# A sandwich of a gated linear-attention block and a mixture of experts: two small GpSimd writes moved behind the making of the shares

## The chip, the cores and the metric

One NeuronCore of one Trainium2 chip runs the whole program in one launch. Its engines work side by side, each through its own instructions in a fixed order: TensorE (PE, matrix products and transposes), VectorE (DVE), ScalarE (ACT), GpSimd (POOL) and SyncE (SP, which mostly issues transfers). They wait for each other through semaphores. The metric is the device time of the program in microseconds (us); lower is better.

## The reference

2048 tokens of 256 channels go through two layers, each wrapped in the same way: the input is normalised, the layer is applied, its output is normalised and added to the input.

```python
x = x + _layernorm(attention_block(_layernorm(x)))     # 16 heads, gated memory along the tokens, then a gated MLP of 1024
x = x + _layernorm(moe(_layernorm(x)))

def moe(x):                                            # E = 8 experts of width 176, top 2; a shared expert of width 704
    shared = (silu(x @ sw_gate) * (x @ sw_up)) @ sw_down
    probs = softmax(x @ router_w.T)
    top_w, top_i = top_k(probs, 2);  top_w = top_w / sum(top_w)
    routed = sum over the two chosen experts e of top_w * ((silu(x @ w_gate[e]) * (x @ w_up[e])) @ w_down[e])
    return routed + sigmoid(x @ shared_gate_w) * shared
```

All of it is in float32.

## The kernel before

**Tiles.** The tokens are cut into `NB` = 8 blocks of 256; in a tile, 128 partitions hold `NT` = 2 groups of 128 tokens each. A block passes through small functions in turn: `enter` (first normalisation), `project`, `remember` and `leave` (the attention block; `leave` holds the second layernorm, `ln2_stats` and `ln2_norm`), `perceptron` (its MLP, eight chunks of the hidden width), `route` (normalisation ahead of the experts, choice of experts, places of the rows) and `shared` (the shared expert).

**The order around the change.** The functions of all blocks are cut into steps, and each step gets a place on one long line; the steps are sorted by place and recorded in that order, so that about four blocks are in work at a time. A recording layer then orders the instructions of each engine; it may put one earlier than it was written, where its data allow. Where the author wants none of that, `behind(engines)` (L107) holds what is recorded within it behind the last instruction recorded so far on these engines: an order edge on the same engine, without a semaphore.

**The route of a block.** `route(b)` makes the rows that go to the experts. Its tile `ln` (L761, tag `ln3`) has only two buffers, so block b + 2 uses the buffer of block b. A row has 339 columns: column 0 the number of the token's first pair (a pair is a token and one of its experts), column 1 the first expert, column 2 the share of the first expert, then the 256 normalised channels (from `X0`), 64 columns of the shared expert's tail (from `T0`), and 16 columns of zeros (from `ROW`). Who writes them:

- L764, ScalarE: the channels, by `normalize`
- L795, GpSimd: the copy of `first_pair` into column 0; L796, GpSimd: the memset of the last 16 columns
- L797, GpSimd: the share from `th`, a tanh on ScalarE; L798, GpSimd: the gate of the shared expert from the same `th`
- L800, GpSimd: the tail, `end` times the gate
- L805, GpSimd: the expert's number from `idf`

Then VectorE and TensorE count places, `rows` (L836) holds the row of each pair in the DRAM tensor `xs`, and four indirect transfers that GpSimd issues (L840) scatter the tile's rows there. When all blocks are through, the experts run over `xs` in 36 blocks of 128 rows (`routed`), scatter their results to `ys`, and the closing part adds all up.

**What else GpSimd does at that time.** It makes the inverse roots of the normalisations: `scale_of` (L328) adds the epsilon (L333) and takes the power -0.5 (L334) of a variance that VectorE has made (L322, L323). `normalize` (L337) goes on from there with a small product on VectorE (L341) and two activations on ScalarE (L343). GpSimd also adds the first layer's output to the input (L737) and clears a part of the experts' weights (L1134).

**What TensorE does.** In the stretch where the change lies its order is a dense row of products of `perceptron` (L389 into `psM`, L714 into `psD`) and `shared` (L389 into `psS` and `psA`), with transposes (L380) between. `psM` has three banks, which ScalarE and VectorE clear (L724, L725, and L767 for the transposes of `route`).

Of the kernel before, what the change touches and what calls it, by code (L numbers as in the profile page):

```python
# [16 lines left out]
DVE, POOL = mybir.EngineType.DVE, mybir.EngineType.Pool  # L17
# [10 lines left out]
def kernel(ctx: ExitStack, tc: tile.TileContext, a: dict, out: bass.AP):  # L28
    nc = tc.nc
# [16 lines left out]
    NT = TB // P  # L46
# [42 lines left out]
    ROW, H0 = T0 + TAIL, T0 - I  # L89
# [6 lines left out]
    first_pair = const.tile([P, NB * NT], F32, name="first_pair")  # L96
# [10 lines left out]
    def behind(*engines):  # L107

        traced, held = nc.cur_bb.bb.instructions, ExitStack()
        for engine in engines:  # L110
            last = next((i for i in reversed(traced) if i.engine == engine), None)
            if last is not None:
                held.enter_context(tc.issue_after(last))
        return held
# [643 lines left out]
    def route(b):  # L758

        t = live[b]  # L760
        ln = act.tile([P, NT, W], F32, tag="ln3", name=f"ln3_{b}", bufs=2)  # L761
# [30 lines left out]
        nc.vector.tensor_copy(th[:, :, 1], lg[:, :, E])  # L792
        nc.scalar.activation(th, th, AF.Tanh, scale=0.5)
        gate = small.tile([P, NT], F32, tag="gate", name=f"gate_{b}", bufs=NB)
        nc.gpsimd.tensor_copy(ln[:, :, 0], first_pair[:, b * NT : (b + 1) * NT])  # L795
        nc.gpsimd.memset(ln[:, :, ROW:], 0.0)  # L796
        nc.gpsimd.tensor_scalar(ln[:, :, 2], th[:, :, 0], 0.5, 0.5, ALU.mult, ALU.add)  # L797
        nc.gpsimd.tensor_scalar(gate, th[:, :, 1], 0.5, 0.5, ALU.mult, ALU.add)  # L798

        nc.gpsimd.tensor_tensor(  # L800
            ln[:, :, T0:ROW], end, gate.unsqueeze(2).to_broadcast([P, NT, TAIL]), ALU.mult
# [239 lines left out]
    def evenly(n):  # L1041
# [12 lines left out]
    runs = (  # L1054
        (perceptron, 3, (*range(NF), 7.8, 7.9, 8.6)),
        (route, 4, (1.4, 2.0, 4.2, 5.2, 5.3, 9.2, 10.2, 10.3)),
        (shared, NB + .9, evenly(NS + 3)),
    )
# [23 lines left out]
    for line in opening.split():  # L1082
        name, b = line.rsplit(":", 1) if ":" in line else (line, "0")
# [149 lines left out]
```

## Time and profile before

| | us |
|---|---|
| median of 3 runs | 529.25 (526.84 to 529.47) |
| the profiled execution | 530.06 |
| its span, first to last instruction | 528.2 |
| TensorE busy | 508.6 |
| VectorE busy | 331.4 |
| ScalarE busy | 216.9 |
| GpSimd busy | 171.5 |
| mean granted clock of TensorE | 0.991 |

The profile names operations by line of the kernel, engine, and tiles as `out<-in`. A timeline row is start, length, engine, line and operation; the brackets at its end give how long the engine sat idle before, and what ended that. The instructions of the two moved lines took 0.183 to 0.675 us (L795, median 0.186, 8 of them) and 0.117 to 0.129 us (L796, median 0.118, 8 of them). By the engine's waits, GpSimd waited ahead of L795 three times for scatters (11.4 us in all, the longest 6.0), twice with TensorE's product named last (3.7) and once with nothing named (2.0).

Where GpSimd has them in the profiled execution, with the block whose tile is written:

| block | L795 at us | what stands right ahead on GpSimd | the block's L805 at us |
|---|---|---|---|
| 0 | 51.24 | memset L302 | 127.90 |
| 1 | 107.94 | root L334 | 164.70 |
| 2 | 153.40 | scatters of block 0 | 200.76 |
| 3 | 188.42 | scatters of block 1 | 237.28 |
| 4 | 224.59 | scatters of block 2 | 267.75 |
| 5 | 257.90 | scatters of block 3 | 303.85 |
| 6 | 294.22 | scatters of block 4 | 339.34 |
| 7 | 329.73 | scatters of block 5 | 364.47 |

The memset L796 follows the copy at once; only block 0's stands apart, at 4.69 us, between the first two steps of the first normalisation.

### The profile page before, as it was taken

How to read it: one execution, taken by the hardware profiler on the slowest of the kernel's cores; microseconds unless marked ns; L12 is line 12 of the kernel's file. 1: busy time of each engine (PE TensorE's matmuls, PEld its weight loads, DVE VectorE, ACT ScalarE, POOL GpSimd, SP SyncE). 2: the span in 40 equal slices, each digit the busy share in tenths (PEclk: the TensorE clock that was granted, in tenths of full speed). 3: DMA queues.
4: the chain of work that ended last, by engine and by line, in shares of the span. 5: the costliest groups of instructions: out<-in, count | busy, mean ns of one | idle time of the engine just before them, and what ended most of it. 6: DMA issues, size and time to landing. Idle time of an engine off the chain costs nothing.

```text
span 528.2 us, 7925 instructions
## 1 busy us (share of the span) xinstructions
PE 508.6 (96%) x2468; PEld 423.1 (80%) x2468; DVE 331.4 (63%) x1100; ACT 216.9 (41%) x500; POOL 171.5 (32%) x309
## 2 busy tenths in 40 slices
PE   8999899999999999999899899999999999999992
PEld 5877687888878888888688788888877777778881
DVE  4788999887896997996754233235134444441983
ACT  4655454544644645543232323213124444443250
POOL 7233202213344341412314214025104334432551
PEclk9999999999999999999999999999999999999997
DMA  4981101001011001110102911002624344323621
GB/s 135 389 264 22 20 2 20 1 1 21 1 54 20 27 27 22 53 20 3 53 1 85 311 26 53 1 0 77 169 67 122 108 120 123 106 85 117 258 87 54
DMA packets 31793, 41.26 MB, mean 78 GB/s; under 512 B 4825, under 2 KB 26629, under 8 KB 31751
## 3 DMA queue, kind: packets, MB, share of 16 engines
q1 hardware_dynamic: 27888, 30.96, 20.5%
q0 software_dynamic: 3584, 9.79, 5.6%
q8 instruction: 20, 0.33, 0.3%
q14 instruction: 23, 0.18, 0.1%
q10 hardware_dynamic: 278, 0.01, 0.0%
HBM read 24.28 MB, written 15.15 MB: 75 GB/s over the span
## 4 chain that ended last, share of the span: by engine, by line
PE 44%; DVE 2%; POOL 2%; DMA 1%; issue 1%; ACT 1%; POOLq 0%; DVEq 0%
PE psM L389 19%; PE psD L389 7%; PE psA L389 6%; PE psS L389 4%; PE psD L714 3%; PE psA L950 1%; PE psB L978 1%; DMA xs<-ln,rows 1%; PE psB L389 1%; POOL xs L840 1%; POOL ln_rs L334 1%; DVE ln_st L322 0%; POOL x L737 0%; POOL ln_rs L333 0%; ACT h L343 0%
## 5 line engine op out<-in xcount | busy, mean ns | idle before, releaser
L389 PE MATMUL psM<-h2T,w_gate 128*128 128x256 f32 x256 | 67.5, 386 | 0.0
L389 PE MATMUL psM<-h2T,w_val 128*128 128x256 f32 x256 | 66.5, 381 | 0.0
L714 PE MATMUL psD<-w_out,hid 128*128 128x256 f32 x256 | 64.3, 381 | 0.1
L989 POOL DMA_INDIRECT ys<-yb,pair x36 | 35.4, 983 | 74.6 <-ACT yb L988 73.3
L389 PEld LDWEIGHTS psM<-h2T,w_gate 128*128 128x128 f32 x256 | 48.2, 192 | 8.3 <-DVE o L635 1.3
L389 PEld LDWEIGHTS psM<-h2T,w_val 128*128 128x128 f32 x256 | 49.0, 192 | 6.7
L714 PEld LDWEIGHTS psD<-w_out,hid 128*128 128x128 f32 x256 | 48.2, 190 | 7.4 <-DVE hid L725 1.2
L389 PE MATMUL psM<-m_w,xT 128*128 x144 | 48.7, 460 | 0.3 <-issue 0.3
L724 ACT ACTIVATE hid<-psM 128x256 f32<-128x256 f32 x64 | 23.7, 376 | 49.6 <-PE psM L389 49.5
L333 POOL TENSOR_SCALAR ln_rs<-ln_mv 128x2 f32<-128x2 f32 (+1 forms) x33 | 8.8, 268 | 104.4 <-DVE ln_mv L323 94.5
L725 DVE TENSOR_TENSOR hid<-hid,psM 128x256 f32<-128x256 f32 x64 | 26.1, 411 | 21.5 <-ACT hid L724 20.9
L840 POOL DMA_INDIRECT xs<-ln,rows x32 | 32.3, 1008 | 15.8 <-issue 7.2
L389 PE MATMUL psD<-m_w,hT 128*128 x144 | 37.2, 381 | 0.0
L389 PEld LDWEIGHTS psM<-m_w,xT 128*128 128x128 f32 x144 | 24.6, 191 | 8.2 <-issue 0.6
L389 PE MATMUL psA<-yT,s_gu 128*128 128x256 f32 x128 | 30.8, 381 | 0.0
L952 DVE COPY xT<-psA 128x256 f32<-128x256 f32 x36 | 15.3, 424 | 24.1 <-PE psA L950 24.1
L974 DVE TENSOR_TENSOR xb<-xb,psM 128x176 f32<-128x176 f32 x36 | 12.2, 338 | 26.9 <-ACT xb L973 26.9
L334 POOL TENSOR_TENSOR ln_rs<-ln_rs,neg_half 128x2 f32<-128x2 f32 (+1 forms) x33 | 26.0, 789 | 2.2
L389 PEld LDWEIGHTS psD<-m_w,hT 128*128 128x128 f32 x144 | 24.6, 191 | 2.4 <-ACT yb L988 0.5
L389 PEld LDWEIGHTS psA<-yT,s_gu 128*128 128x128 f32 x128 | 23.9, 190 | 3.0
L973 ACT ACTIVATE xb<-psM 128x176 f32<-128x176 f32 x36 | 11.4, 317 | 32.7 <-PE psM L389 31.8
L988 ACT ACTIVATE yb<-psD,share 128x256 f32<-128x256 f32 x36 | 17.0, 473 | 18.6 <-PE psD L389 18.4
(269 smaller groups left out, 1065.8 us busy)
## 6 DMA issues: line engine op xcount, KB each, us to landing
xb<-xs SPq DMA_DIRECT2D x36, 169.5 KB
g<-ys SPq DMA_DIRECT2D x8, 512.0 KB
xs<-zeros SPq DMA_DIRECT2D x16, 169.5 KB
x<-in_L_attn_x_dram SPq DMA_DIRECT2D x8, 256.0 KB
decay<-by_head SPq DMA_DIRECT2D x14, 128.0 KB
out_dram<-f SPq DMA_DIRECT2D x7, 256.0 KB
m_w<-in_L_ffn_w_gate_dram SPq DMA_DIRECT2D x2, 704.0 KB
m_w<-in_L_ffn_w_up_dram SPq DMA_DIRECT2D x2, 704.0 KB
```

What stands on the lines that cost most here:

```text
L333: nc.gpsimd.tensor_scalar(rs, mv[:, :, 1], EPS, None, ALU.add)
L334: roots.append(nc.gpsimd.tensor_tensor(rs, rs, neg_half[:, 0:nt], ALU.pow).ins)
L389: nc.tensor.matmul(po, lhs[i], rhs[i], start=(i == 0), stop=(i == len(lhs) - 1))
L714: nc.tensor.matmul(total[:, n * C : (n + 1) * C], hids[f][:, tok(n)], w_out[:, f, :], start=(f == 0 and n == 0), stop=(f == NF - 1 and n = ...
L724: nc.scalar.activation(hid, po[:, 0:TB], AF.Silu)
L725: nc.vector.tensor_tensor(hid, hid, po[:, TB:], ALU.mult)
L840: inst = nc.gpsimd.indirect_dma_start(out=xs, out_offset=bass.IndirectOffsetOnAxis(ap=rows[:, c : c + 1], axis=0), in_=ln[:, n, :], in_off ...
L952: nc.vector.tensor_copy(xT, pt[:, 0 : KC * P].rearrange("p (k t) -> p k t", k=KC))
L973: nc.scalar.activation(h[:, 0:I], po[:, 0:I], AF.Silu)
L974: nc.vector.tensor_tensor(h[:, 0:I], h[:, 0:I], po[:, I:GU], ALU.mult)
L988: nc.scalar.activation(yb, po[:, 0:C], AF.Copy, scale=share)
L989: inst = nc.gpsimd.indirect_dma_start(out=ys, out_offset=bass.IndirectOffsetOnAxis(ap=pair, axis=0), in_=yb, in_offset=None, bounds_check= ...
```

## The change

The copy L795 and the memset L796 are written behind the two makings L797 and L798, and inside `behind(POOL)`: the recording layer may not put them ahead of the gate of the same block.

```diff
         gate = small.tile([P, NT], F32, tag="gate", name=f"gate_{b}", bufs=NB)
-        nc.gpsimd.tensor_copy(ln[:, :, 0], first_pair[:, b * NT : (b + 1) * NT])
-        nc.gpsimd.memset(ln[:, :, ROW:], 0.0)
         nc.gpsimd.tensor_scalar(ln[:, :, 2], th[:, :, 0], 0.5, 0.5, ALU.mult, ALU.add)
         nc.gpsimd.tensor_scalar(gate, th[:, :, 1], 0.5, 0.5, ALU.mult, ALU.add)
+
+        with behind(POOL):
+            nc.gpsimd.tensor_copy(ln[:, :, 0], first_pair[:, b * NT : (b + 1) * NT])
+            nc.gpsimd.memset(ln[:, :, ROW:], 0.0)
 
         nc.gpsimd.tensor_tensor(
             ln[:, :, T0:ROW], end, gate.unsqueeze(2).to_broadcast([P, NT, TAIL]), ALU.mult
```

In the built program GpSimd then has, for each block: L805, L797, L798, the copy, the memset, L800. The wait for the scatters of block b - 2, which read the same buffer, stands at L805, now the first writer of the tile on GpSimd. TensorE, VectorE, ScalarE and SyncE have the same instructions in the same order with the same waits. (Lines below the change are two higher in the new program; the texts use the old numbers unless they say otherwise.)

## The prediction

> **What bounds the kernel now.** I read the page first (busy shares), then TensorE's own timeline for its idle time, then GpSimd's timeline around the moved lines, then the granted clock in one-microsecond stretches.
>
> ```profile
> PE 508.6 (96%) x2468; PEld 423.1 (80%) x2468; DVE 331.4 (63%) x1100; ACT 216.9 (41%) x500; POOL 171.5 (32%) x309
> ```
>
> TensorE sets the time: it is busy for 508.6 of 528.2 us, and its order is fixed. Every other engine matters only where TensorE stands still for it. Outside the first 90 us and the end it does so in few places; these five rows of its timeline (start, length, operation, and in brackets the idle time before and who ended it) are nearly all of it:
>
> ```profile
> 260.02 0.33 PE L380 MATMUL psB<-ident,ln 128*128 128x128 f32 x1 [1.20 <-ACT ln L343]
> 260.51 0.55 PE L380 MATMUL psB<-ident,ln 128*128 128x128 f32 x3 [0.16 <-ACT ln L343]
> 261.81 1.65 PE L389 MATMUL psM<-s_gu,yT 128*128 128x137 f32 x8 [0.75 <-DVE hid L725]
> ...
> 296.05 0.70 PE L389 MATMUL psA<-s_down,shid 128*128 128x256 f32 x2 [0.27 <-DVE shid L865]
> 297.89 0.70 PE L389 MATMUL psA<-s_down,shid 128*128 128x256 f32 x2 [1.15 <-DVE shid L865]
> ```
>
> Two places, which I call A (1.20 + 0.16 + 0.75 = 2.11 us) and B (0.27 + 1.15 = 1.42 us). What stood behind them is in GpSimd's timeline:
>
> ```profile
> 254.93 0.96 POOL L840 DMA_INDIRECT xs<-ln,rows  x1 [0.30 <-issue]
> 257.90 0.18 POOL L795 COPY ln<-first_pair 128x2 f32<-128x2 f32 x1 [2.00 <-issue]
> 258.02 0.12 POOL L796 MEMSET ln<- 128x32 f32 x1
> 258.12 0.22 POOL L333 TENSOR_SCALAR ln_rs<-ln_mv 128x2 f32<-128x2 f32 x1
> 258.42 0.72 POOL L334 TENSOR_TENSOR ln_rs<-ln_rs,neg_half 128x2 f32<-128x2 f32 x1
> ...
> 287.26 0.96 POOL L840 DMA_INDIRECT xs<-ln,rows  x1 [0.30 <-issue]
> 294.22 0.18 POOL L795 COPY ln<-first_pair 128x2 f32<-128x2 f32 x1 [6.00 <-DMA xs<-ln,rows]
> 294.35 0.12 POOL L796 MEMSET ln<- 128x32 f32 x1
> 294.44 0.22 POOL L333 TENSOR_SCALAR ln_rs<-ln_mv 128x2 f32<-128x2 f32 x1
> 294.74 0.72 POOL L334 TENSOR_TENSOR ln_rs<-ln_rs,neg_half 128x2 f32<-128x2 f32 x1
> ```
>
> The copy L795 of block b + 2 stands right behind the four scatters (L840) of block b. It writes the tile that they read (`ln3` has two buffers), so GpSimd waits until they have landed: 2.00 us at A, 6.00 us at B, where the experts' weights load at 339 GB/s (290 to 294). Queued behind the copy is the root of the second layernorm (L333, L334). Its input was ready: the statistics L323 ended at 255.50 and 287.20. Behind the root wait L341 on VectorE, L343 on ScalarE (idle 5.79 and 8.14 us until then) and, behind those, what frees TensorE.
>
> **The lost clock.** After the restart at A the granted clock (the column behind POOL's) falls to a half:
>
> ```profile
> 262.00:263.00 1.00, 1.00 (x7) 1.00 (x7) 0.96 (x2) 0.00 (x0) 0.00 (x0) 0.68 0.00 0
> 263.00:264.00 1.00, 1.00 (x5) 0.91 (x4) 0.94 (x2) 0.00 (x0) 0.00 (x0) 0.50 0.00 0
> 264.00:265.00 1.00, 1.00 (x4) 0.72 (x4) 0.77 (x2) 0.46 (x1) 0.00 (x0) 0.50 0.00 0
> 265.00:266.00 1.00, 1.00 (x4) 0.82 (x3) 0.77 (x2) 1.00 (x3) 0.00 (x0) 0.61 0.03 8
> ```
>
> That is 0.32 + 0.50 + 0.50 + 0.39 = 1.71 us of work not done. The chain of waits says much the same: the 16 matmuls from 261.81 take 4.58 us there, while 8 of the narrow kind take 0.93 and 8 of the wide kind 1.73 elsewhere; 4.58 - 2.66 = 1.92. I take 1.8.
>
> **The change, part by part.** Nothing is added or removed; in the built programs the four other engines keep order and waits, and on GpSimd the two instructions of each of the 8 blocks move from early places to between L798 and L800.
>
> *Root at A.* With the copy gone, L333 starts after the last scatter's issue, 255.89. No row shows a computation right behind an indirect scatter. The nearest are the 0.30 us between two scatters, and L252, which starts 0.03 us behind the plain DMA L185 (6.27 to 6.79) while that is still under way (it lands 2.1 to 2.7 us after issue). So L333 starts at 255.92 to 256.19 instead of 258.12: 1.93 to 2.20 earlier, say 2.06. The restart hangs on it link by link (L334, L341, L313 to L315, L635, L636, L725 end to end from 258.42 to 261.66), so it moves from 261.81 to 259.75. TensorE's earlier work ends at 258.82 and four transposes take 0.44 to 0.60, so about 0.4 us idle remain, and the restart is not cut short. Gain 2.06.
>
> *Clock at A.* If the half clock came of the gap, 0.4 us in place of 2.11 is not enough for it: B's 1.42 us left the clock at 1.00. Gain 1.8. VectorE does not become the bound behind it: the hid of the last tile is ready at 269.86 and used at about 272.3; shifted by 2.06 and by 3.86 that leaves 0.6 us.
>
> *Root at B.* The scatter's issue ends at 288.22, so L333 starts at about 288.4 instead of 294.44, and L343 ends at about 290.7 instead of 296.78. TensorE ran on until 295.8 without that work, so ScalarE and VectorE have 5 us to catch up. All 1.42 us go; the lower end, if they catch up badly, is 0.7.
>
> *The other six blocks.* Block 2's copy waited 3.61 us at 153.4, but TensorE was busy there (19.93 of the 20 us from 144 to 164). At 188.42 and 224.59 the root behind the copy waited 0.8 to 0.9 us more for VectorE. At 329.73 nothing follows until 339.34, and at 51.24 and 107.94 nothing waited. L796 at 4.69 stands in an opening that TensorE waits for; it may give 0.07. All these: 0.
>
> *Where the two land.* Copy 0.19 + memset 0.12 = 0.30 us lie ahead of L800, at worst the largest ever seen, 0.68 + 0.13 = 0.8. Behind L800 GpSimd is idle for 2.2 us in the last block (the scatter waits for `rows`) and 3.9 to 10 us in the others. That idle time hides it; uncovered it would cost 8 x 0.30 = 2.4 us. The wait for the scatters of block b moves to L805 of block b + 2; block 4's landed by 294.1 and block 6's L805 comes at 339.34, and in the others at least 30 us lie between, so it costs nothing. ScalarE's L343 into that tile waits for the same scatters in both programs.
>
> *What comes after.* All later work shifts as a whole: the first rows `xb` are asked for at 378.99 and used at 388.97, and this chain starts from TensorE's own router products, so it moves along.
>
> **Sum.** 2.06 + 1.8 + 1.42 = 5.3 us; the bounds are 1.93 + 1.7 + 0.7 = 4.3 and 2.20 + 1.9 + 1.42 + 0.07 = 5.6. The profiled execution took 530.06 us (span 528.2, 1.86 around it): 524.8. The median of the runs, 529.25, is 0.81 below it; from there 524.0. One of the runs took 526.84, so part of what I remove may be missing in some executions. I take 524.5.
>
> **Rivals.**
> *The drop of the clock is not of this gap* and stays, or was not there in most runs. For it: TensorE's idle time is only 2.11 us, broken by transposes. Against: the drop follows the restart at once, and nothing like it is seen elsewhere between 90 and 480 us. Gain 2.06 + 1.42 = 3.5: 526.6 by the profiled execution, 525.8 by the median. [...]
> *GpSimd is not free until the scatter has landed*, whatever stands behind it, so the edit does not do what it says. For it: every computation behind a scatter in this trace waited, though each was the copy itself. Against: L252 behind L185. Then only copy and memset leave the path, 0.22 us at each place (257.90 to 258.12): 0.4 us, 528.9 to 529.7.
> *A new wait takes the old one's place:* TensorE gains at A, and ScalarE, in order, holds it at the next bank. VectorE is busy for most of 259 to 270, which speaks for it; half the gain, 527.
> *Slower:* the two instructions ahead of L800 delay the scatters, and through them the last block's rows. Price 0.30 to 0.8 a block, 2.4 to 6.4 in all if each were on the path and the roots brought nothing: 531.7 to 535.7 from the median. It decides only where GpSimd has less than 0.3 us idle behind L800; the least is 2.2.
>
> **How the numbers follow.** Forecast 0.60 (523.2 to 525.8), clock rival 0.15, new wait 0.10, GpSimd held 0.08, slower 0.07. The range runs over the forecast, the clock rival and most of the new wait: 522.8 to 527.8. About 0.5% (2.65 us, bound 526.6 and 531.9) is what a measurement can tell from no change. Faster: 0.60 + most of the clock rival 0.12 = 0.72; slower 0.06; the rest, 0.22, within.
>
> **What would show it.** L333 within 0.3 us of the last L840 at both places; no idle time of TensorE over 0.5 us between 250 and 300; clock 1.00 throughout there; L800 0.3 us later against L798 with no one waiting. Wrong if L333 still starts 2 us or more behind L840, if the half clock turns up at another place, or if the idle time of TensorE reappears before 389 us.

## The result, and the profile after

| | before | after |
|---|---|---|
| median of 5 runs each, side by side | 527.11 us (526.84 to 529.47) | 523.39 us (523.27 to 523.42) |
| ratio, 95% interval | 1 | 0.991 (0.9885 to 0.9934) |
| the profiled execution | 530.06 | 523.42 |
| its span | 528.2 | 521.3 |
| TensorE busy | 508.6 | 505.0 |
| mean granted clock of TensorE | 0.991 | 0.996 |

The change saves 0.9%, 3.7 us between the medians. The profiled executions differ by more, 6.6 us. The runs of the program before explain the difference. They fall into two groups, here three at 526.8 to 527.1 and two at 529.3 to 529.5. The runs after the change lie within 0.15 us of each other. What separates the groups is worked out below; the profiled execution of before belongs to the longer one.

Line numbers of after below: L795 and L796 are the two makings (L797, L798 before), L799 the copy, L800 the memset, L802 the tail (L800 before), L807 the expert's number (L805 before), L842 the scatters (L840 before).

The page of after, busy times:

```profile
PE 505.0 (97%) x2468; PEld 421.7 (81%) x2468; DVE 331.7 (64%) x1100; ACT 217.5 (42%) x500; POOL 169.6 (33%) x309
```

TensorE's busy time fell by 3.6 us although it has the same 2468 instructions: a part of the gain is work that runs at a higher clock (0.996 on the mean against 0.991). TensorE's own timeline of after, the rows with idle time ahead of them from 140 us to 372 us:

```profile
258.50 1.17 PE L389 MATMUL psM<-s_gu,yT 128*128 128x137 f32 x8 [0.40 <-DVE hid L725]
...
370.73 1.97 PE L389 MATMUL psM<-yT,s_gu 128*128 128x256 f32 x8 [0.45 <-ACT shid L866]
```

Of the five rows before, one is left, and its 0.40 us stands for the three rows at A (2.11 us); the two rows at B have gone. The row at 370.73 was there before as well. GpSimd's timeline of after, at A, at B, and where the moved lines of block 5 now stand; the last row is the first write of block 6's tile:

```profile
253.79 0.96 POOL L842 DMA_INDIRECT xs<-ln,rows  x1 [0.30 <-issue]
254.78 0.24 POOL L333 TENSOR_SCALAR ln_rs<-ln_mv 128x2 f32<-128x2 f32 x1
...
282.29 0.96 POOL L842 DMA_INDIRECT xs<-ln,rows  x1 [0.30 <-issue]
283.28 0.24 POOL L333 TENSOR_SCALAR ln_rs<-ln_mv 128x2 f32<-128x2 f32 x1
...
296.90 0.21 POOL L807 COPY ln<-idf 128x2 f32<-128x2 f32 x1 [10.82 <-DVE idf L806]
297.18 0.19 POOL L795 TENSOR_SCALAR ln<-th 128x2 f32<-128x2 f32 x1
297.33 0.20 POOL L796 TENSOR_SCALAR gate<-th 128x2 f32<-128x2 f32 x1
297.48 0.18 POOL L799 COPY ln<-first_pair 128x2 f32<-128x2 f32 x1
297.60 0.12 POOL L800 MEMSET ln<- 128x32 f32 x1
297.68 0.40 POOL L802 TENSOR_TENSOR ln<-end,gate 128x128 f32<-128x128 f32 x1
...
332.40 0.21 POOL L807 COPY ln<-idf 128x2 f32<-128x2 f32 x1 [11.44 <-DVE idf L806]
```

The root L333 starts 0.03 us after the last scatter's issue ends (253.79 + 0.96 = 254.75; 282.29 + 0.96 = 283.25) where it started 2.2 and 6.2 us after it. The instruction that now writes the tile first, L807, waits for VectorE in both blocks and no longer for a scatter. The clock after the restart at A, in windows of 2 us (length, busy time and count of PE, PEld, DVE, ACT, POOL, then granted clock, DMA share, GB/s):

```profile
262.00:264.00 2.00, 2.00 (x11) 1.77 (x10) 1.93 (x15) 1.04 (x3) 0.00 (x0) 1.00 0.02 4
264.00:266.00 2.00, 2.00 (x11) 1.74 (x11) 2.00 (x12) 0.75 (x3) 1.44 (x6) 1.00 0.00 0
```

The half clock of 262.4 to 265.8 is gone.

**Where the 6.9 us between the two spans went.** The marks are TensorE's restarts near 64 us, at A and near 371 us, and GpSimd's first scatters of blocks 1 and 4 (181.56 and 283.30 before, 180.40 and 278.33 after):

| stretch | before | after | less |
|---|---|---|---|
| first 64 us | 64.05 | 63.36 | 0.69 |
| 64 us to block 1's scatters | 117.51 | 117.04 | 0.47 |
| from these to the restart at A | 80.25 | 78.10 | 2.15 |
| from A to 21 us on (half clock before) | 21.49 | 19.83 | 1.66 |
| from there over B to TensorE's row near 371 | 94.37 | 92.40 | 1.97 |
| from there to the end | 150.53 | 150.57 | 0.0 |

Of the first two rows, 1.2 us, about 0.9 us also lies between two executions of one and the same program (experiment 1 below); no run shows that the rest is the change's. The next three rows, A, the half clock and B, are the change's, the half clock only in some executions.

### The profile page after: what moved, and what is told of

Its sections match the earlier page's. It is cut to its first block, busy times and chain, and to the rows that moved or that the text cites. A ratio compares the mean times of both kernels' runs of the same rounds, so it can differ in the third digit from the quotient of the medians.

```text
span 521.3 us, 7930 instructions
## 1 busy us (share of the span) xinstructions
PE 505.0 (97%) x2468; PEld 421.7 (81%) x2468; DVE 331.7 (64%) x1100; ACT 217.5 (42%) x500; POOL 169.6 (33%) x309
## 4 chain that ended last, share of the span: by engine, by line
PE 82%; DVE 12%; POOL 2%; issue 1%; ACT 1%; DMA 1%; POOLq 0%; DVEq 0%
PE psM L389 35%; PE psA L389 17%; PE psD L714 9%; PE psD L389 7%; PE psS L389 5%; PE psB L389 3%; PE psA L952 2%; PE psB L980 2%; DVE ln_st L322 1%; DVE mem L611 1%; PE psB L380 1%; POOL ln_rs L334 1%; DVE hid L725 1%; DVE sm L373 1%; PE psM L380 1%
## 5 line engine op out<-in xcount | busy, mean ns | idle before, releaser
L333 POOL TENSOR_SCALAR ln_rs<-ln_mv 128x2 f32<-128x2 f32 (+1 forms) x33 | 8.6, 260 | 106.5 <-DVE ln_mv L323 92.7
L842 POOL DMA_INDIRECT xs<-ln,rows x32 | 32.3, 1010 | 15.7 <-issue 7.2
```

The costliest lines, as they stand in the source:

```text
L842: inst = nc.gpsimd.indirect_dma_start(out=xs, out_offset=bass.IndirectOffsetOnAxis(ap=rows[:, c : c + 1], axis=0), in_=ln[:, n, :], in_off ...
```

## The experiments

Beside each of these kernels the program before ran on the same chip, in three sets: 63 executions of it in all. The granted clock splits them: 33 have 0.993 or more and took 526.78 to 527.94 us (median 527.24); 30 have 0.991 or less and took 528.44 to 530.82 (median 529.14). The shares differ from set to set (14 long of 29, 5 of 17, 11 of 17), so a median of before can fall in either group, and the groups of a kernel are given with it.

### 1. Order in the text without the edge

The two lines are written behind the makings, but not inside `behind(POOL)`.

```diff
-        with behind(POOL):
-            nc.gpsimd.tensor_copy(ln[:, :, 0], first_pair[...])
-            nc.gpsimd.memset(ln[:, :, ROW:], 0.0)
+        nc.gpsimd.tensor_copy(ln[:, :, 0], first_pair[...])
+        nc.gpsimd.memset(ln[:, :, ROW:], 0.0)
```

> The two writes are moved behind the shares in the text, but without the order edge; the recording layer then puts them where they were, and the program is the one before, instruction for instruction. So this is the kernel before, timed again. Theory 1 (the half clock after gap A comes in some executions only): two groups of times, about 527.0 and 529.4, 2.4 apart, the longer ones with a granted clock near 0.991, the shorter ones near 0.995. Rival (the profiled execution of 530.06 was the rule, and 526.84 a stray): nearly all times near 529.3 with one clock.

Measured: ratio 1.0003 (0.9986 to 1.0019), 12 executions, 5 at 527.2 to 528.0 and 7 at 528.6 to 529.6. The built program is that of before, instruction by instruction: the recording layer puts the two lines early again. So the edge alone makes the change, and this kernel is a second look at before. Its start of 63.71 us, against 64.05 in the profile of before, and 36.22 us between the scatters of blocks 0 and 1, where that profile has 36.77 and after has 36.22, show that the first two rows of the table are mostly what one execution differs from another by. (With A alone, experiment 2, where block 0's memset still stands early, the start took 63.47 us, 0.11 more than after; executions of one program differ by more than that.) Its TensorE and its clock at A:

```profile
259.15 0.33 PE L380 MATMUL psB<-ident,ln 128*128 128x128 f32 x1 [1.23 <-ACT ln L343]
259.64 0.55 PE L380 MATMUL psB<-ident,ln 128*128 128x128 f32 x3 [0.16 <-ACT ln L343]
260.94 2.17 PE L389 MATMUL psM<-s_gu,yT 128*128 128x137 f32 x8 [0.76 <-DVE hid L725]
```

```profile
262.00:264.00 2.00, 2.00 (x8) 1.82 (x8) 1.83 (x4) 0.34 (x1) 0.00 (x0) 0.52 0.00 0
```

The profiled execution, 528.8 us, is of the long group, and it has the half clock: eight products take 2.17 us, 0.27 each.

### 2 and 3. Place A alone, place B alone

The edge for one block only: block 5, whose copy stood behind block 3's scatters, and block 6, whose copy stood behind block 4's.

```diff
+        held = b == 5          # b == 6 in the other kernel
+        if not held:
             nc.gpsimd.tensor_copy(...); nc.gpsimd.memset(...)
         nc.gpsimd.tensor_scalar(ln[:, :, 2], ...)
         nc.gpsimd.tensor_scalar(gate, ...)
+        if held:
+            with behind(POOL):
+                nc.gpsimd.tensor_copy(...); nc.gpsimd.memset(...)
```

> The two writes are held back for block 5 alone, the one at place A. Theory 1: TensorE's idle time at A falls from 2.1 us to about 0.4 and the half clock behind it is gone in every execution; the gap at B stays at 1.2 to 1.4. Against the executions of before without the half clock (527.0) a gain of about 1.9 to 2.2: 525.0; against those with it about 4. Rival (the clock falls for another reason): times in two groups again, 525 and 527.

> Held back for block 6 alone, the one at place B. Theory 1: the idle time at B is gone, 1.4 to 2.0 us gained, and A stays as it was with its two groups of times: 525.2 and 527.6. Rival (B's idle time comes back at the next wait of TensorE): under 0.5 us gained.

Measured: A alone 525.09 us (6 executions, 524.66 to 525.26, one group), ratio 0.9937 (0.9915 to 0.9959). B alone 526.87 us (12 executions), ratio 0.996 (0.9943 to 0.9977), again in two groups, 5 at 525.1 to 525.4 and 7 at 526.8 to 527.6. TensorE's timeline with A alone, and then with B alone:

```profile
258.58 1.17 PE L389 MATMUL psM<-s_gu,yT 128*128 128x137 f32 x8 [0.39 <-DVE hid L725]
...
292.51 0.70 PE L389 MATMUL psA<-s_down,shid 128*128 128x256 f32 x2 [1.15 <-DVE shid L871]
```

```profile
258.91 0.33 PE L380 MATMUL psB<-ident,ln 128*128 128x128 f32 x1 [1.03 <-ACT ln L343]
259.40 0.55 PE L380 MATMUL psB<-ident,ln 128*128 128x128 f32 x3 [0.16 <-ACT ln L343]
260.70 1.17 PE L389 MATMUL psM<-s_gu,yT 128*128 128x137 f32 x8 [0.76 <-DVE hid L725]
...
372.93 1.97 PE L389 MATMUL psM<-yT,s_gu 128*128 128x256 f32 x8 [0.45 <-ACT shid L870]
```

Each edit removes its own gap and leaves the other. The two groups go with the gap at A: where it is closed, no execution is long; where it is open, some are. The sizes, against the short group of before in all sets (527.24): A 2.15, B 1.9. Both together, the change: 527.24 - 523.39 = 3.85, near their sum of 4.05 (with A already closed, B adds 525.09 - 523.39 = 1.70). Against the long group it is 529.14 - 523.39 = 5.75; the difference, 1.9 us, is the half clock. These differences partly cross sets. Against the short group of their own sets, A is 2.06 (527.15) and the change 3.57 (three executions, median 526.96), so the sizes are good to about 0.3 us.

### 4. Block 2 alone

Its copy waited 3.61 us for scatters in before, more than A's.

```diff
+        held = b == 2
```

> Held back for block 2 alone, where the copy waited 3.6 us and TensorE stood still for nothing that the timeline shows. Theory of the prediction: no gain, 526.8 to 529.5 as before. Rival (the profile of after shows all work behind this place 0.5 us earlier, so TensorE was slowed there without an idle row): 0.4 to 0.6 us gained, in the profile a shift between 150 and 180 us and in the median.

Measured: ratio 0.9999 (0.9982 to 1.0017), 12 executions, 7 at 527.2 to 527.5 and 5 at 528.8 to 529.5. GpSimd's timeline shows the wait gone, with another work there in its place, and TensorE's shows A as it was:

```profile
150.35 0.22 POOL L528 TENSOR_SCALAR eq<-ssq 128x32 f32<-128x32 f32 x1 [1.14 <-DVE rm L309]
```

```profile
258.73 0.33 PE L380 MATMUL psB<-ident,ln 128*128 128x128 f32 x1 [1.01 <-ACT ln L343]
259.22 0.55 PE L380 MATMUL psB<-ident,ln 128*128 128x128 f32 x3 [0.16 <-ACT ln L343]
260.52 1.17 PE L389 MATMUL psM<-s_gu,yT 128*128 128x137 f32 x8 [0.76 <-DVE hid L725]
```

```profile
262.00:264.00 2.00, 2.00 (x11) 1.77 (x10) 1.54 (x4) 0.76 (x2) 0.00 (x0) 1.00 0.00 0
```

The wait of 3.61 us on GpSimd, at a place where TensorE was busy for 19.93 of 20 us, was worth nothing here. The last rows tell more: this profiled execution, 527.37 us, has nearly the gap of experiment 1 (1.93 us against 2.15) and keeps the clock at 1.00; eight products take 1.17 us.

### 5. The copy alone

```diff
         nc.gpsimd.memset(ln[:, :, ROW:], 0.0)
...
+        with behind(POOL):
+            nc.gpsimd.tensor_copy(ln[:, :, 0], first_pair[...])
```

> Only the copy of the pairs' numbers is held back; the memset of the last columns stays where it was. Theory (what counts is which instruction on GpSimd writes the tile first, for this one takes the wait for the scatters): the memset now waits, the roots at A and B start as late as before less about 0.1 us, and the times stay in the two groups of before, 527.0 and 529.2. Rival (it is the copy, with its 0.19 to 0.68 us, that costs): a gain of more than 1 us.

Measured: ratio 0.9991 (0.9978 to 1.0003), 12 executions, 9 at 526.5 to 527.3 and 3 at 528.2 to 528.6. GpSimd at A (here L842 is the scatter and L795 the memset):

```profile
254.04 0.96 POOL L842 DMA_INDIRECT xs<-ln,rows  x1 [0.30 <-issue]
256.89 0.12 POOL L795 MEMSET ln<- 128x32 f32 x1 [1.88 <-issue]
256.98 0.22 POOL L333 TENSOR_SCALAR ln_rs<-ln_mv 128x2 f32<-128x2 f32 x1
```

The memset takes over the wait, 1.88 us for 2.00: in both programs it is the first instruction on GpSimd to write the recycled tile that waits, the copy in before and the memset here. Holding back the copy without the memset gives about 0.2 us at most.

### 6. More work ahead of the tail

The rival on the slower side: eight more copies of 128x2 stand between the memset and the tail in every block.

```diff
         with behind(POOL):
             nc.gpsimd.tensor_copy(...); nc.gpsimd.memset(...)
+            for _ in range(8):
+                nc.gpsimd.tensor_copy(ln[:, :, 0], first_pair[...])
+        with behind(POOL):
-        nc.gpsimd.tensor_tensor(ln[:, :, T0:ROW], end, gate..., ALU.mult)
+            nc.gpsimd.tensor_tensor(ln[:, :, T0:ROW], end, gate..., ALU.mult)
```

> The changed kernel with eight more copies of the same column in each block, held between the memset and the product that makes the tail, so that the product and all behind it on GpSimd come 0.9 to 1.5 us later in every block: three to five times the delay that the change itself brings. Theory (the idle time behind the product covers it, 2.2 us in the last block and more in the others): 523.4, at most 0.3 more. Rival (the delay reaches the scatters and the last block's rows): 1 us and more, up to 8 x 1.2 = 9.6.

Measured: 523.18 us (4 executions, 522.98 to 523.40), ratio 0.9916 (0.9893 to 0.9939): no slower than the change. GpSimd in the last block, first with the copies (L805 is the tail, L845 the scatter), then after:

```profile
358.56 1.97 POOL L802 COPY ln<-first_pair 128x2 f32<-128x2 f32 x8
360.48 0.73 POOL L805 TENSOR_TENSOR ln<-end,gate 128x128 f32<-128x128 f32 x1
361.49 1.04 POOL L845 DMA_INDIRECT xs<-ln,rows  x1 [0.28 <-POOL ln L805]
```

```profile
360.86 1.09 POOL L842 DMA_INDIRECT xs<-ln,rows  x1 [2.12 <-DVE ends L911]
```

The copies take 1.9 to 2.3 us in each block, over six times what the change puts there. They delay the last block's first scatter by 0.6 us and the end not at all.

### 7 to 9. A gap at A made by GpSimd's own work

Is it the length of the gap that drops the clock, or the scatter traffic beside it? On top of the change, N memsets of 128x2 stand ahead of the root at A. No DMA is waited for.

```diff
+        if part == "B" and b_now[0] == 7:      # the root at A
+            with behind(POOL):
+                for _ in range(N):              # 10, 16 or 34
+                    nc.gpsimd.memset(warm, 0.0)
+            with behind(POOL):
+                nc.gpsimd.tensor_scalar(rs, mv[:, :, 1], EPS, None, ALU.add)
```

> The changed kernel with ten small memsets ahead of the root at place A alone, about 1 us. Theory (TensorE's restart at A hangs on this root one to one, and the half clock needs a gap near 2 us): the restart comes about 1 us later, idle time there about 1.4 us, clock 1.00, one group of times at 524.4. Rival (the half clock comes of any gap, by chance): part of the executions 1.7 us longer.

> The same with 34 memsets, about 3 us or a little more. Theory: the restart comes 3 us later, idle time about 3.4 us, 526.4; the longer gap brings the half clock in most executions or all, not in a half of them as before: 528.2. Rival (the fall of the clock has nothing to do with the gap's length): it comes in a half of the executions or in none, 526.4 for those without.

> The changed kernel with 16 memsets ahead of the root at place A (each took 0.15 us in the run with ten), about 2.2 us: the root starts as late against the scatters as in the kernel before, but GpSimd is busy and not waiting for a transfer. Theory (the half clock follows the length of the gap and nothing else): idle time at A about 2.1 us and the half clock in a part of the executions, as before: two groups of times, 525.6 and 527.4. Rival (the fall has to do with the wait for the scatters or with their traffic): one group at 525.6.

| N | memsets, us | median us (executions) | ratio (95%) | groups |
|---|---|---|---|---|
| 10 | 1.52 | 525.01 (6) | 0.9952 (0.9934 to 0.9971) | one, no half clock |
| 16 | 2.47 | 527.10 (12) | 0.9957 (0.9941 to 0.9973) | 5 at 525.6 to 525.9, 7 at 527.0 to 527.5 |
| 34 | 5.32 | 531.0 (6) | 1.0063 (1.0044 to 1.0082) | 529.6 to 531.5, all with half clock |

GpSimd's timeline with 10, and the restart of TensorE:

```profile
254.65 1.52 POOL L339 MEMSET warm<- 128x2 f32 x10
256.14 0.22 POOL L341 TENSOR_SCALAR ln_rs<-ln_mv 128x2 f32<-128x2 f32 x1
```

```profile
259.84 1.17 PE L399 MATMUL psM<-s_gu,yT 128*128 128x137 f32 x8 [0.75 <-DVE hid L735]
```

The root starts 1.36 us later than after (256.14 against 254.78), TensorE 1.34 (259.84 against 258.50): one for one, as the chain of links says. The clock with 16, in windows of 1 us:

```profile
262.00:263.00 1.00, 1.00 (x4) 0.89 (x4) 0.93 (x3) 0.00 (x0) 0.00 (x0) 0.50 0.00 0
263.00:264.00 1.00, 1.00 (x4) 0.73 (x3) 0.90 (x2) 0.34 (x1) 0.00 (x0) 0.50 0.00 0
```

With no wait for a DMA in it, a gap of the old length has the half clock again, and in the same two groups. With 34, TensorE idles 4.28 us in one piece. The mean clock of every execution (0.986 to 0.991) is that of the drop:

```profile
262.16 0.33 PE L390 MATMUL psB<-ident,ln 128*128 128x128 f32 x1 [4.28 <-ACT ln L353]
```

Only the fastest of them, 529.59 us, was profiled, and it has one drop. The others are up to 1.9 us longer at a lower clock; whether they had a second one isn't shown. I had reckoned 34 memsets at about 3 us; they took 5.3 (0.156 each), so this run says less about where the drop begins than it was meant to, and N = 16 was run for that.

**When the drop comes.** An idle time of one length brings the drop in some executions and not in others: with 1.93 us of it the clock stayed at 1.00 in the profile of block 2 alone, with 1.86 us it fell in that of the copy alone. The profiles show what it went with. In each of them the clock falls once more after TensorE's last work (in before at 521.78, where the last product ends at 518.41). In the five that have the half clock at A, the fall there and the one at the end are 259.41 us apart (before, the order without the edge, the copy alone, 34 memsets) or 256.00 us (16 memsets). The half clock at A lasts 3.41 us (262.36 to 265.78 in before), and the two distances are 76 and 75 steps of 3.413 us. In the order without the edge the half clock runs from 260.51 to 263.92 (columns as above):

```profile
260.10:260.50 0.40, 0.09 (x1) 0.00 (x0) 0.40 (x2) 0.40 (x2) 0.00 (x0) 1.00 0.00 0
260.52:260.92 0.40, 0.00 (x0) 0.01 (x1) 0.40 (x2) 0.09 (x1) 0.00 (x0) 0.50 0.00 0
263.50:263.90 0.40, 0.40 (x3) 0.31 (x2) 0.40 (x2) 0.24 (x1) 0.00 (x0) 0.50 0.00 0
263.94:264.34 0.40, 0.40 (x4) 0.35 (x3) 0.02 (x1) 0.40 (x2) 0.00 (x0) 1.00 0.00 0
```

So in these five profiles the changes of the clock lie on a grid of 3.413 us. It lies elsewhere against the program from execution to execution: the fall comes 0.55 us behind TensorE's restart in before (262.36 and 261.81) and 0.43 us ahead of it in the order without the edge (260.51 and 260.94). The drop went with how much of the idle time lies in one step. In the order without the edge the step that ends at 260.51 began at 257.10, ahead of the gap, and holds 1.23 + 0.16 + 0.33 = 1.72 us of it. Where a profile has no half clock at A, the grid is counted back from the fall at the end. With B alone, from 517.75, it has borders at 258.33 and 261.75. The first of them falls into the gap and leaves 1.49 us in the next step; the clock stays at 1.00. For each kernel, TensorE's idle time at A in the profile, the most of it that lies in one step, the clock there, and how many of all executions have the half clock (by their times and mean clock; only one execution of each kernel was profiled):

| kernel | idle at A, us | most in one step, us | clock in the profile | with half clock |
|---|---|---|---|---|
| the change | 0.40 | 0.40 | full | 0 of 5 |
| 10 memsets | 1.38 | 0.75 | full | 0 of 6 |
| block 2 alone | 1.93 | 1.07 | full | 5 of 12 |
| B alone | 1.95 | 1.49 | full | 7 of 12 |
| the copy alone | 1.86 | 1.59 | half | 3 of 12 |
| order without the edge | 2.15 | 1.72 | half | 7 of 12 |
| 16 memsets | 2.32 | 1.82 | half | 7 of 12 |
| before | 2.11 | 1.99 | half | 30 of 63 |
| 34 memsets | 4.90 | 2.98 | half | 6 of 6 |

The third column puts all nine in order, full clock up to 1.49 us and half clock from 1.59 us; the second does not. From these nine profiles the shares can be estimated: with a border of 1.54 us and a grid that lies anywhere with the same chance, the profiled gap of before has the drop in 46% of all executions (measured 30 of 63), that of B alone in 42% (7 of 12), that of the copy alone in 39% (3 of 12), that of 10 memsets in none and that of 34 in all. That border of 1.5 to 1.6 us is one of this place, with the transposes in the gap counted as work. Counted as idle, they bring the step of the copy alone to 2.47 us; whether they count as work for the clock no run here separates. At the end of the program a step with 1.80 us of idle time brought no fall (the change) and one with 2.06 us did (16 memsets).

### 10 and 11. The root ahead of the scatters

The opposite remedy: leave the copy where it is and let the root pass. In before, and once more on top of the change, the four scatters of blocks 3 and 4 are held until the root has been recorded ahead of them; `behind_root` does that for block 6 already.

```diff
+                late_root = part is route and b in (3, 4) and place >= at[6]
+                if late_root:
+                    place += 0.7
                 step = lambda run=run: next(run, None)
+                if late_root:
+                    step = lambda run=step: behind_root(run)
```

> The kernel before, the copy and the memset where they were, but the scatters of blocks 3 and 4 held behind the root that stood behind the copy: on GpSimd the order at A and B is root, scatters, copy, memset. The other engines keep their order. Theory (the copy's wait costs only because the root is queued behind it): the copy still waits 2 and 6 us and nobody minds; one group of times at the changed kernel's 523.4, or 0.3 below. Rival (the wait costs something of its own, or the scatters come too late): between 524 and 529.

> The same order of root and scatters in the changed kernel. The root's input is ready at 254.35 and L333 starts at 254.78 there, so 0.35 us of TensorE's remaining 0.40 us of idle time at A go: 523.0 to 523.1, which is less than a measurement tells from 523.4. At B nothing more. Rival (the scatters, 1 us later, hold something up): 523.4 or more.

Measured: in before 523.04 us (5 executions), ratio 0.9896 (0.9873 to 0.9918); on the change 523.06 us (5), ratio 0.9896 (0.9874 to 0.9918). GpSimd's timeline of the first, old line numbers:

```profile
254.74 0.22 POOL L333 TENSOR_SCALAR ln_rs<-ln_mv 128x2 f32<-128x2 f32 x1 [5.31 <-DVE rw L314]
...
260.75 1.14 POOL L840 DMA_INDIRECT xs<-ln,rows  x1 [0.30 <-issue]
263.95 0.25 POOL L795 COPY ln<-first_pair 128x2 f32<-128x2 f32 x1 [2.06 <-PE psM L389]
...
287.37 0.96 POOL L840 DMA_INDIRECT xs<-ln,rows  x1 [0.30 <-issue]
294.01 0.19 POOL L795 COPY ln<-first_pair 128x2 f32<-128x2 f32 x1 [5.68 <-DMA xs<-ln,rows]
```

The copy still waits 2.06 and 5.68 us, nearly what it waited in before, and the kernel is as fast as with the change: the cost was never the wait but the root queued behind it. The two remedies don't add up, since each removes the same cost; the idle row of 0.40 us at A goes as well. Both medians lie 0.3 us below that of the change, but these were measured in another set, and that small a difference between sets isn't shown.

Not tried: a third buffer for the tile, which would take away the wait itself.

## Why the prediction was right, and where it was not

**The mechanism** held at each link. The root stood behind the copy, the copy behind the scatters (experiments 5, 10); A and B are worth something each and together about the whole (2, 3), and block 2, with a longer wait than A's, nothing (4).

**Root at A, gain 2.06:** 2.15 between the profiles, 2.15 from A alone. Its open point, whether GpSimd computes right behind an indirect scatter, was bounded at 0.03 to 0.30 us; it is 0.03. The 0.4 us that should be left of the gap are the 0.40 in the trace.

**Clock at A, gain 1.8: this is the step that failed.** It read: "If the half clock came of the gap, 0.4 us in place of 2.11 is not enough for it: B's 1.42 us left the clock at 1.00. Gain 1.8." The size is right: 1.66 between the profiles, 1.9 between the groups. That the drop comes of the gap is right as well, and the first rival, by which it does not, falls with experiments 2 and 7 to 9. But the sum counted the drop as if every execution of before had it. It was in 30 of 63, about the 46% that experiments 7 to 9 estimate from the idle time in one step of the grid. Taken against the short group, the change is worth 3.85 us, and there is no 1.8 in that; the median of five runs beside the change, 527.11, is of the short group. The sum also started from a median of three runs, two of which were of the long group. The prediction saw the one run at 526.84 and said that a part might be missing in some executions, but kept the term whole. Weighted by 30 of 63 it is 0.9 us.

**Root at B, gain 1.42, as low as 0.7:** too small. B measured 1.97 between the profiles, 1.9 alone and 1.70 on top of A. The sum took the rows' idle time, 1.42, for the whole loss. These are the ten products at B, first in before, where the two rows that the prediction shows (296.05 and 297.89) follow this one, then in after:

```profile
294.32 1.46 PE L389 MATMUL psA<-s_down,shid 128*128 128x256 f32 x6
```

```profile
289.32 2.32 PE L389 MATMUL psA<-s_down,shid 128*128 128x256 f32 x10
```

In before they take 4.27 us from first to last (294.32 to 298.59), in after 2.32; the difference is 1.95. Of this 1.42 is idle time, and 0.54 is that the three rows of before are longer together than the one of after (1.46 + 0.70 + 0.70 = 2.86). In the unbroken row of after each product starts about 0.22 us after the one before it, though its record is 0.38 us long; at each of the two stops of before this overlap is lost, and the first product behind the stop takes 0.48 us.

**What the errors make of the time.** The forecast of 524.5 was 1.1 us too high. B was short by 0.3 to 0.5 us, and the base, a mixture of the two groups with one execution at 530.06, was too high for the rest. That the time still came within about 1 us is partly luck: the base held the half clock that the sum then took away in full. The gain, reckoned at 5.3 us, was 3.7 between the medians, and by groups 3.85 or 5.75. (527.24 - 2.15 - 1.70 = 523.39 is no test of the parts, since 2.15 and 1.70 are differences between these same medians.)

**The two writes ahead of the tail, and the moved wait, 0:** right. Experiment 6 charges six times the price and loses nothing, so the slower rival falls. L807 of blocks 5 and 6 waits for VectorE (10.82 and 11.44 us).

**GpSimd held until a scatter has landed:** falls by the 0.03 us between L842 and L333 at both places. (Not every row behind a scatter in before was the copy, as the prediction says: L805 at 364.47 is one, and it waited for VectorE.) **A new wait in the old one's place:** none; TensorE's next row with idle time after A is at 370.73, which was there before.

## What to carry to other kernels

When an engine with a fixed order waits for a transfer, ask what is queued behind the waiting instruction; here the first writer of a recycled buffer carried that wait (the copy 2.00 us in before, the memset 1.88 us in experiment 5), so move all early writers behind the urgent work, or the urgent work ahead of what they wait for, which came to the same here. A wait that had nothing urgent behind it (3.6 us in block 2, 5.7 us in experiment 10) cost nothing here. Before a drop of the clock goes into a sum, look at several executions: one profile shows whether it happened, not how often. And the idle rows at B understated what the stops in a dense row of products cost: 1.42 us of them stood for 1.95.

## What the runs showed of the hardware

- In the five profiles with two falls of TensorE's clock these lie on a grid of 3.413 us (259.41 or 256.00 us apart), which lies elsewhere against the program from execution to execution. At A the clock fell to a half when 1.59 us or more of idle time lay in one step (five profiles) and not at 1.49 us or less (four), and the half clock lasted one step in each of the five.
- So a gap of 1.9 to 2.3 us brought the drop in 59 of 123 executions, one of up to 1.4 us in 0 of 11, one of 4.9 us in 6 of 6. Where it came in a part of the executions, the times of the kernel fell into two groups about 0.4% apart (1.5 to 2.1 us between their medians). Whether GpSimd waited for a DMA or ran memsets meanwhile made no difference that these runs show.
- Ten products that ran 2.32 us in an unbroken row took 4.27 us with two stops in it, 0.54 us more than the idle time of the stops.
- After the change GpSimd's root started 0.03 us after the issue of the last indirect scatter had ended, at A and at B. What was held until the scatters had landed was the instruction that writes their tile (2.00 and 6.00 us before the change), and with it the root queued behind it.
- On GpSimd 34 memsets of 128x2 in a row took 5.32 us, 0.156 each, and 8 copies of 128x2 took 1.97, 0.25 each.
